# Four-layer graph network on one core: layer 2's normalisation moves from VectorE to ScalarE, under new due times

## The chip, the cores and the metric

The kernel runs on one core of one Trainium2 chip. The metric is device time in microseconds (us) of one execution. The engines are TensorE (PE in the profile; PEld is its weight load), VectorE (DVE), ScalarE (ACT), GpSimd (POOL) and the DMA queue of SyncE (SP).

## What is computed

There are 16 graphs ("batches") of 1024 nodes with 128 features, and an integer adjacency matrix for each. Four layers follow, each behind a layer norm with ReLU and with a residual sum. Cut to what matters here:

```python
# layer 0: two products with the row-softmaxed transposed adjacency, two batch norms over all batches
h = relu(layernorm(x));  x = x + L0(h, adj, ...)
# layer 1: graph attention
h = relu(layernorm(x));  Wh = h @ W.T
e = leaky_relu((Wh @ a_src)[:, :, None] + (Wh @ a_dst)[:, None, :], 0.2)
x = x + softmax(where(adj == 0, -inf, e)) @ Wh
# layer 2: attention by dot products of the nodes, weighted by one vector for each edge type
h = relu(layernorm(x))
e = leaky_relu(einsum('bid,bjd,dk->bkij', h, h, A), 0.2)   # the type in adj picks k
x = x + softmax(scores) @ h
# layer 3: graph attention like layer 1, with elu on its result
```

The layer norm is `(x - m) / sqrt(v + 1e-5)` over the 128 features of a node. Layer 0 needs statistics over all batches, so it is finished for all of them before layer 1 can start for any. Layers 1 to 3 are independent from batch to batch.

## The kernel before

Nodes lie on the 128 partitions, so a batch is 8 blocks of 128 nodes. `first_layer`, `load_weights` and `norms` make up the first stage (some 370 us), `plain_layers` the second, with layers 1 to 3 of all batches. `general_stack` is a second branch for other edge types and is not taken with these inputs.

The order of the work is not written by hand. Each function registers steps with a planner (`Plan`): an engine, a guessed cost in us, the tiles that it reads and writes, and the closure that issues its instructions. `Plan.attempt` lists the steps along a modelled timeline: an engine takes, among the steps that could start within `WITHIN` us of the earliest, the one with the lowest rank, and the rank is the batch's due time minus the length of the longest path behind the step. `Plan.emit` then issues all steps in that order. A due time belongs to a batch, and there are two lists: `L0_DUES` for the first stage and `DUES` for the second. They were found by search. Tiles come from small pools ("rooms"); a step that opens a room takes the one that has been free longest. Each engine runs its instructions in the order of issue, so whatever waits holds up everything behind it on the same engine.

The steps of a batch in `plain_layers`, with their lines before the change:

- Load `gt_rows`, `x` and the adjacency `at` (L855, L844, L841). Three batches kept from the first stage have theirs already. There are four `at` tiles: at0 to at2 and atc0. The last part of layer 0 is added by L882, L887 and L891.
- `norm(scaled)`: statistics of the nodes (L904), aggregates (L910), then on GpSimd `va = var + eps` and `rs = va ** -0.5` (L915, L916). For layers 1 and 3 (`scaled` false) the nodes are centred with ReLU on ScalarE by L929, with the negated mean (L912) as a bias column; the factor `rs` is applied later. For layer 2 (`scaled` true) they are centred and scaled on VectorE by L926. TensorE turns the blocks (L933), ScalarE copies them out of PSUM (L936; with ReLU in layer 2).
- `gat(layer, ext)` for layers 1 and 3: a product with the weights (L1004), scores (L1009), exponentials (L1017). The scores of the nodes are turned into a row (L1024), copied by L1027, sent to DRAM by L1030 and fetched from there into all partitions (`ub`, L1033). For layer 1 of the three kept batches L1042 and L1046 spread them without the round trip. L1060 writes the values `v`. Eight weighings of 128x1024 follow on VectorE (L1068), each into one of ten `q` tiles (named xg6 to xg15), and eight product steps on TensorE (L957).
- Layer 2: `ha` from the turned nodes (L1081), the values by a ReLU of `y` (L1084). Row block by row block there are dots on TensorE (L1100), two exponentials each on ScalarE (L1108, L1104), the larger of both (L1118) and a mask (L1121) on VectorE. Only the upper triangle is computed; the lower one is turned (L1132) and masked (L1136). Then the products (L957).
- Layers 1 and 2 end with reciprocals of the sums (L975), a scaling on ScalarE (L981) and the residual (L993). Layer 3 ends with L1150, L1156 and two joins (L1160, L1162), and the store (L1170).

Of the kernel before, what the change touches and what calls it, by code (L numbers as in the profile page):

```python
# [14 lines left out]
AF = mybir.ActivationFunctionType  # L15
ALU = mybir.AluOpType
# [23 lines left out]
    419.5, 419.5,  # L40
], 0.1
DUES, WITHIN = [
    18.0, 41.8, 62.8, 59.8, 76.6, 100.4, 120.4, 141.2, 164.8, 183.8, 204.1, 225.0, 245.7, 269.5, 265.9, 272.2,
], 0.05
GAT_LIMIT = 30.0
DOT_KEEP = 60.0
DOT_LIMIT = 110.0
# [16 lines left out]
class Plan:  # L64
# [11 lines left out]
    def room(self, kind):  # L76
        return Room(kind)
# [132 lines left out]
def groups_of(n, k):  # L210
    return [range(a, min(a + k, n)) for a in range(0, n, k)]
# [576 lines left out]
def plain_layers(tc, q_tiles, x, out, adj_t, gt_rows, u_rows, ident, ident_h, mhalf, gat1, gat3, edge, shift,  # L788
                 kcs, q9_all, rows9, held, kept):
    nc = tc.nc  # L790
# [7 lines left out]
    with ExitStack() as ctx:  # L798
# [31 lines left out]
        room = plan.room  # L830

        def batch(b):
            seat = room("seat")

            def step(engine, us_, run, reads=(), writes=(), moved=0, also=()):
                plan.step(engine, us_, run, reads, writes, moved, b, (seat, *also))
# [12 lines left out]
            X = [(xr, n) for n in range(NB)]  # L849

            def xs(n, m=None):
                return xr.ap.rearrange("p (k d) -> p k d", d=D)[:, n if m is None else slice(n, m), :]
# [44 lines left out]

            def norm(scaled):
                st, mv, va, rs, y, gt = (room(k) for k in ("st", "mv", "col", "col", "y", "gt"))
                nm = None if scaled else room("col")  # L900
                for ns in TRI:
                    def stats(ns=ns):
                        for n in ns:
                            nc.vector.bn_stats(st.ap[:, n, :], xs(n))  # L904

                    step("dve", 0.2 * len(ns), stats, [X[n] for n in ns], [(st, n) for n in ns])

                def aggregate():
                    for n in range(NB):
                        nc.vector.bn_aggr(mv.ap[:, n, :], st.ap[:, n, :])  # L910
                    if not scaled:
                        nc.vector.tensor_scalar_mul(nm.ap, mv.ap[:, :, 0], -1.0)  # L912

                def power():
                    nc.gpsimd.tensor_scalar_add(va.ap, mv.ap[:, :, 1], LN_EPS)  # L915
                    nc.gpsimd.tensor_tensor(rs.ap, va.ap, mhalf, ALU.pow)  # L916

                step("dve", 0.7, aggregate, [(st, n) for n in range(NB)], [mv] if scaled else [mv, nm])
                step("pool", 2.1, power, [mv], [va, rs])
                for js in groups_of(NB, 4):  # L920
                    ps = room("ps")

                    def centre(js=js):
                        for n in js:
                            if scaled:
                                nc.vector.tensor_scalar(y.ap[:, n, :], xs(n), mv.ap[:, n, 0:1],  # L926
                                                        rs.ap[:, n : n + 1], ALU.subtract, ALU.mult)
                            else:
                                nc.scalar.activation(y.ap[:, n, :], xs(n), AF.Relu, bias=nm.ap[:, n : n + 1])  # L929

                    def turn(js=js, ps=ps):
                        for k, n in enumerate(js):
                            nc.tensor.transpose(ps.ap[:, k * P : (k + 1) * P], y.ap[:, n, :], ident)  # L933

                    def relu(js=js, ps=ps):
                        nc.scalar.activation(gt.ap[:, js[0] * P : (js[-1] + 1) * P], ps.ap,  # L936
                                             AF.Relu if scaled else AF.Copy)

                    if scaled:
                        step("dve", 0.84, centre, [X[n] for n in js] + [mv, rs], [(y, js[0])])  # L940
                    else:
                        step("act", 1.0, centre, [X[n] for n in js] + [nm], [(y, js[0])])
                    step("pe", 0.44, turn, [(y, js[0])], [ps], also=[gt])
                    step("act", 0.54, relu, [ps], [(gt, js[0])])
                return y, gt, rs
# [50 lines left out]

            def gat(layer, ext):
                y, gt, rs = norm(False)
                sc, ex, er, v, ub = (room(k) for k in ("tri", "tri", "col", "v", "ub"))
                parts = [room("ps") for _ in TRI]  # L1000
# [74 lines left out]
            finish(gat(1, gat1))  # L1075

            y, ht, _ = norm(True)
            ha, h1 = room("gt"), room("h1")

# [597 lines left out]
```

## Time and profile before

| | us |
|---|---|
| median of 3 runs | 1424.29 (1423.61 to 1425.9) |
| the profiled execution | 1423.44 |
| its span in the profile | 1421.6 |
| TensorE busy | 1373.0 |
| VectorE busy | 1100.7 |
| ScalarE busy | 794.2 |
| GpSimd busy | 358.9 |

The profile is of one execution. Its span leaves out 1.84 us of the device time. A line such as L957 is a line of the kernel before. Matmuls are pipelined and their ends are modelled, so the mean duration of one is longer than the distance from one to the next: a product step of layers 1 to 3 has 16 records and takes 1.79 us in an unbroken run. The groups give "busy, mean duration of one", then the idle time of the engine just ahead of them and what ended most of it. The waits give "engine and tile that waited, line <- who released it: us in total, times, longest".

### The profile page before, as it was taken

How to read it: one execution, taken by the hardware profiler on the slowest of the kernel's cores; microseconds unless marked ns; L12 is line 12 of the kernel's file. 1: busy time of each engine (PE TensorE's matmuls, PEld its weight loads, DVE VectorE, ACT ScalarE, POOL GpSimd, SP SyncE). 2: the span in 40 equal slices, each digit the busy share in tenths (PEclk: the TensorE clock that was granted, in tenths of full speed). 3: DMA queues.
4: the chain of work that ended last, by engine and by line, in shares of the span. 5: the costliest groups of instructions: out<-in, count | busy, mean ns of one | idle time of the engine just before them, and what ended most of it. 6: DMA issues, size and time to landing. Idle time of an engine off the chain costs nothing.

```text
span 1421.6 us, 30420 instructions
## 1 busy us (share of the span) xinstructions
PE 1373.0 (97%) x11710; PEld 1262.9 (89%) x11710; DVE 1100.7 (77%) x3148; ACT 794.2 (56%) x2123; POOL 358.9 (25%) x469
## 2 busy tenths in 40 slices
PE   4999999999999999999999999999999999999997
PEld 3889899899898898998899898998989998998897
DVE  4877666454688889887889788887888798977786
ACT  3766766666545645636374645546374655346643
POOL 7877676562210110201011101101011111020000
PEclk9999999999999999999999999999999999999999
DMA  9999887870300002121111112021221110000011
GB/s 157 146 186 170 116 167 149 112 99 7 119 2 16 31 31 75 46 90 60 46 60 46 64 41 75 31 80 47 84 60 60 60 46 31 31 1 16 16 44 65
DMA packets 56379, 99.05 MB, mean 70 GB/s; under 512 B 6328, under 2 KB 45600, under 8 KB 52896
## 3 DMA queue, kind: packets, MB, share of 16 engines
q1 hardware_dynamic: 37504, 79.17, 15.8%
q0 software_dynamic: 18720, 17.83, 14.5%
q8 instruction: 94, 1.54, 0.4%
q14 instruction: 61, 0.50, 0.1%
HBM read 118.37 MB, written 28.95 MB: 104 GB/s over the span
## 4 chain that ended last, share of the span: by engine, by line
PE 82%; DVE 8%; ACT 4%; POOL 2%; DMA 2%; issue 1%; DVEq 0%; ACTq 0%; POOLq 0%
PE psc L957 43%; PE psc L1100 7%; PE psa L499 7%; PE psa L459 7%; PE gram L352 4%; PE psc L1004 3%; PE psc L1132 3%; PE psc L933 2%; PE psa L418 2%; PE psc L882 1%; DVE xg L1068 1%; DMA a<-in_adj_dram 1%; DVE eu L1118 1%; ACT y L929 1%; POOL hv L398 1%
## 5 line engine op out<-in xcount | busy, mean ns | idle before, releaser
L957 PE MATMUL psc<-v,xg 128*128 128x129 f32 x4096 | 482.6, 275 | 1.3 <-DVE xg L1068 1.2
L957 PEld LDWEIGHTS psc<-v,xg 128*128 128x128 f32 x4096 | 471.7, 192 | 13.1 <-issue 7.3
L957 PEld LDWEIGHTS psc<-h,xg 128*128 128x128 f32 x2048 | 239.1, 192 | 16.9 <-DVE xg L1136 8.9
L957 PE MATMUL psc<-h,xg 128*128 128x129 f32 x2048 | 247.9, 276 | 3.8 <-DVE xg L1136 3.3
L915 POOL TENSOR_SCALAR col<-mv 128x8 f32<-128x8 f32 x48 | 20.9, 434 | 868.1 <-DVE mv L910 800.8
L1068 DVE SCALAR_TENSOR_TENSOR xg<-ub,tri,at 128x1024 f32<-128x1024 f32 x176 | 217.5, 1276 | 4.3 <-DMA at<-adj_t 2.9
L1108 ACT ACTIVATE eu<-psc,edge_shift 128x512 f32<-128x512 f32 x192 | 113.6, 592 | 173.5 <-PE psc L1100 173.0
L426 ACT ACTIVATE at<-psa 128x1024 fp8e4<-128x1024 fp8e4 x128 | 131.2, 1033 | 45.1 <-PE psa L418 43.3
L1100 PE MATMUL psc<-gt,gt 128*128 128x512 f32 (+3 forms) x384 | 150.9, 492 | 5.3 <-DVE xg L1136 4.0
L1118 DVE SCALAR_TENSOR_TENSOR eu<-e,edge_shift,eu 128x1024 f32<-128x1024 f32 (+7 forms) x128 | 104.0, 812 | 38.0 <-ACT e L1104 36.8
L459 PE MATMUL psa<-hv,a 128*128 128x257 f16 x1024 | 120.7, 277 | 3.3 <-DVE hv L401 3.3
L499 PE MATMUL psa<-rv,at 128*128 128x259 f16 x1024 | 120.0, 275 | 2.7 <-DVE g L506 2.2
L459 PEld LDWEIGHTS <-a 128*128 128x128 fp8e4 x1024 | 101.4, 99 | 19.1 <-issue 3.5
L499 PEld LDWEIGHTS <-at 128*128 128x128 fp8e4 x1024 | 99.6, 98 | 19.1 <-issue 3.6
L929 ACT ACTIVATE y<-xg,col 128x128 f32<-128x128 f32 x256 | 79.1, 400 | 65.1 <-DVE col L912 65.1
L1104 ACT ACTIVATE e<-psc,edge_shift 128x512 f32<-128x512 f32 x192 | 113.6, 592 | 0.0
L1068 DVE SCALAR_TENSOR_TENSOR xg<-ub,tri,atc 128x1024 f32<-128x1024 f32 x80 | 99.2, 1275 | 6.0 <-DMA ub<-u_rows 3.8
L1156 ACT ACTIVATE y<-psc,col 128x128 f32<-128x128 f32 x256 | 69.2, 419 | 56.5 <-DVE col L1150 56.3
L471 POOL TENSOR_SCALAR rv<-r,cola 128x128 f16<-128x128 f32 x128 | 82.0, 650 | 61.2 <-DVE r L467 61.0
L981 ACT ACTIVATE y<-psc,col 128x128 f32<-128x128 f32 x256 | 71.9, 394 | 45.3 <-DVE col L975 39.2
L916 POOL TENSOR_TENSOR col<-col,mhalf 128x8 f32<-128x8 f32 x48 | 94.1, 1961 | 4.0
L1060 ACT ACTIVATE v<-psc,col 128x128 f32<-128x128 f32 x256 | 72.4, 394 | 26.6 <-DVE col L1020 22.8
(209 smaller groups left out, 1941.9 us busy)
## 6 DMA issues: line engine op xcount, KB each, us to landing
a<-in_adj_dram POOLq DMA_DIRECT2D x128, 128.0 KB, 7.2
ub<-u_rows SPq DMA_DIRECT2D x29, 512.0 KB, 4.0
xb<-in_x_dram SPq DMA_DIRECT2D x27, 512.0 KB, 6.8
adj_t<-at SPq DMA_DIRECT2D x13, 1024.0 KB, 4.9
at<-adj_t SPq DMA_DIRECT2D x8, 1024.0 KB
out_dram<-y SPq DMA_DIRECT2D x15, 512.0 KB, 3.9
gt_rows<-xg SPq DMA_DIRECT2D x13, 512.0 KB, 5.6
xg<-gt_rows SPq DMA_DIRECT2D x13, 512.0 KB, 3.9
```

Of the source, the lines that this page charges most:

```text
L426: nc.scalar.activation(at.ap[:, i, :], ps.ap.bitcast(F8)[:, t::2], AF.Square, saturate=False, accum_out=sums.ap[:, i : i + 1])
L459: nc.tensor.matmul(ps.ap[:, : 2 * D + 1], block[:, i % 2 :: 2], hv.ap[:, j, :], start=(j == 0), stop=(j == NB - 1))
L471: nc.gpsimd.tensor_scalar_mul(rv.ap[:, i, 0:D], r.ap[:, i, :D], rc.ap[:, i : i + 1])
L499: nc.tensor.matmul(ps.ap[:, :W2], at.ap[:, i, j * P : (j + 1) * P], rv.ap[:, i, :], start=(i == 0), stop=(i == NB - 1))
L916: nc.gpsimd.tensor_tensor(rs.ap, va.ap, mhalf, ALU.pow)
L929: nc.scalar.activation(y.ap[:, n, :], xs(n), AF.Relu, bias=nm.ap[:, n : n + 1])
L957: nc.tensor.matmul(acc[g].ap[:, k * V1 : (k + 1) * V1], weights[m].ap[:, n * P : (n + 1) * P], values.ap[:, m, :], start=(m == 0 and k == ...
L1068: nc.vector.scalar_tensor_tensor(q[m].ap, ub.ap, ex.ap[:, m, 1:2], at.ap[:, m, :], ALU.max, ALU.mult)
L1100: nc.tensor.matmul(ps.ap[:, : len(c)], ha.ap[:, m * P : (m + 1) * P], ht.ap[:, m * P + c[0] : m * P + c[-1] + 1], start=True, stop=True)
L1104: nc.scalar.activation(e.ap[:, c[0] : c[-1] + 1], ps.ap[:, : len(c)], AF.Exp, bias=shift[:, 0:1], scale=1.0 - SLOPE)
L1108: nc.scalar.activation(eu.ap[:, ROW[m] + c[0] : ROW[m] + c[-1] + 1], ps.ap[:, : len(c)], AF.Exp, bias=shift[:, 1:2], scale=SLOPE)
L1118: nc.vector.scalar_tensor_tensor(t, e.ap[:, :wide], shift[:, 2:3], t, ALU.max, ALU.mult)
```

## The change

In layer 2's norm, a small VectorE operation (`offset`, 128x8) computes `-mean * rs`. The nodes are then centred and scaled by ScalarE, with this as a bias column and `rs` as a scale column, instead of by VectorE's `tensor_scalar`. The step's place in the planner goes from `"dve"` at 0.84 us to `"act"` at 1.0 us, and a step of 0.17 us for the offset is new. `DUES` holds other numbers, and `WITHIN` goes from 0.05 to 0.1. The first stage's due times are the same.

```diff
 DUES, WITHIN = [
-    18.0, 41.8, 62.8, 59.8, 76.6, 100.4, 120.4, 141.2, 164.8, 183.8, 204.1, 225.0, 245.7, 269.5, 265.9, 272.2,
-], 0.05
+    -27.7, 9.3, 14.4, 25.7, 73.9, 96.1, 117.5, 139.4, 159.2, 182.2, 201.8, 221.8, 234.9, 284.6, 296.8, 299.1,
+], 0.1
...
-                nm = None if scaled else room("col")
+                nm = room("col")
...
+                def offset():
+                    nc.vector.scalar_tensor_tensor(nm.ap, mv.ap[:, :, 0], -1.0, rs.ap, ALU.mult, ALU.mult)
+
                 step("dve", 0.7, aggregate, [(st, n) for n in range(NB)], [mv] if scaled else [mv, nm])
                 step("pool", 2.1, power, [mv], [va, rs])
+                if scaled:
+                    step("dve", 0.17, offset, [mv, rs], [nm])
...
                             if scaled:
-                                nc.vector.tensor_scalar(y.ap[:, n, :], xs(n), mv.ap[:, n, 0:1],
-                                                        rs.ap[:, n : n + 1], ALU.subtract, ALU.mult)
+                                nc.scalar.activation(y.ap[:, n, :], xs(n), AF.Identity, bias=nm.ap[:, n : n + 1],
+                                                     scale=rs.ap[:, n : n + 1])
                             else:
                                 nc.scalar.activation(y.ap[:, n, :], xs(n), AF.Relu, bias=nm.ap[:, n : n + 1])
...
                     if scaled:
-                        step("dve", 0.84, centre, [X[n] for n in js] + [mv, rs], [(y, js[0])])
+                        step("act", 1.0, centre, [X[n] for n in js] + [nm, rs], [(y, js[0])])
```

## The prediction

> **What bounds the kernel now.** I read the page's busy shares first.
>
> ```profile
> PE 1373.0 (97%) x11710; PEld 1262.9 (89%) x11710; DVE 1100.7 (77%) x3148; ACT 794.2 (56%) x2123; POOL 358.9 (25%) x469
> ```
>
> TensorE (PE) is busy for 97% of a span of 1421.6 us. Neither engine that the change touches is the bound. What it can win is the time in which PE stands. The windows by stage show where that is: the first layer ends near 362 us, the three later layers fill the rest.
>
> ```profile
> 362.00:400.00 38.00, 35.10 (x331) 34.22 (x331) 29.18 (x134) 24.52 (x68) 10.26 (x20) 0.96 0.33 112
> 600.00:700.00 100.00, 96.87 (x808) 90.74 (x808) 80.27 (x201) 47.29 (x134) 9.02 (x8) 1.00 0.21 69
> 1364.00:1421.60 57.60, 50.40 (x449) 50.19 (x449) 41.93 (x67) 21.72 (x81) 0.00 (x0) 0.97 0.16 57
> ```
>
> The columns are length, then busy time of PE, weight load, DVE, ACT, POOL. From 400 to 1300 us, PE stands 15.2 us in nine windows of 100 us, while DVE is busy 753.6 of 900 us (84%) and ACT 53%. The stretches 362 to 400 and 1300 to 1364 add 2.9 and 1.1 us. The last 7.2 us are the tail behind the last product. The view of PE's waits says who holds it up.
>
> ```profile
> PE psc L1100 <- DVE xg L1136: 4.0, 5, 1.2
> PE psc L957 <- DVE xg L1136: 3.3, 7, 1.1
> PE psc L1132 <- DVE xg L1136: 2.0, 2, 1.1
> PE psc L957 <- DVE xg L1068: 1.2, 3, 0.5
> ```
>
> In the later layers DVE accounts for 11.8 us of waiting (these four rows, and 1.3 us in smaller ones), ACT for 4.3 us. In the chain of waits a product step of 16 records takes 1.79 us when it follows another and 2.05 us when it starts after a wait, so some twenty stalls cost another 0.26 us each, about 5 us. The ceiling is therefore 15.2 + 2.9 + 1.1 + 5 = 24 us, 1.7%.
>
> **Part 1: the eight centring operations of layer 2 go from DVE to ACT.** The groups by line and shape:
>
> ```profile
> L926 DVE TENSOR_SCALAR y<-xg,mv,col 128x128 f32<-128x128 f32 x128 | 34.8, 341 | 6.4 <-POOL col L916 6.4
> L929 ACT ACTIVATE y<-xg,col 128x128 f32<-128x128 f32 x256 | 79.1, 400 | 65.1 <-DVE col L912 65.1
> L463 ACT ACTIVATE t<-psa,level,cola 128x129 f32<-128x129 f32 x128 | 54.6, 460 | 42.2 <-PE psa L459 28.4 <-DVE cola L435 8.9 <-DVE r L467 3.9
> L912 DVE TENSOR_SCALAR col<-mv 128x8 f32<-128x8 f32 x32 | 5.5, 172 | 1.1
> ```
>
> DVE loses 128 operations, 34.8 us in all (0.272 us each). It gains 16 of 128x8, priced by L912: 16 x 0.172 = 2.8 us. Net -32 us: 1101 becomes 1069, and its share from 400 to 1300 us falls from 84% to 81%. ACT gains 128. Below, one costs what L929 costs, with a bias column alone: 79.1/256 = 0.309 us. Above, it costs what L463 costs, with bias and scale columns, though from PSUM and 129 wide: 54.6/128 = 0.427 us. Two columns are what the new operation has, so I take 0.40: +51 us (40 to 55), 794 becomes 845, 59%. A step of four takes 1.6 us instead of 1.09 us.
>
> The Trainium skill, "ScalarE: Activation LUTs", section "What ACT_TABLE_LOAD costs", speaks against the change: it gives an ACTIVATE 186 ns + 0.833 ns an element, about 93 ns more for each per-partition column, and an overlap of 93 ns between neighbours. By that page one new operation would be an estimated 0.39 us, dearer than the 0.272 us it replaces, and ACT's sum +49 us; no row here shows a two-column ACTIVATE from SBUF.
>
> A change of function table is not added: Identity, Square, Copy, Relu and Exp all run now, and the trace has one table load of 1.28 us; the built program has one too.
>
> **Part 2: the new wait.** The offset waits in DVE's queue for GpSimd's power (0.43 + 1.96 us after the aggregates), as the first centring did; that wait cost DVE 6.4 us in 6 places and I leave it at that. Queued behind it are weighings (L1068) and masks. The path from aggregates to the layer's node transposes grows by 0.17 us, two semaphore hops of some 0.05 us, and 0.5 us of slower step: 0.7 to 0.8 us for a batch. The cover is the PE work that the order puts between the last product of layer 1 and those transposes. I counted it in the built order of both programs at the durations of the profile: 14 to 43 us in all batches but two. The first has 9.8 us against a path of some 8.1 (0.17 reciprocal, 2.2 scaling, 0.4 add, 0.5 statistics, 0.64 aggregates, 2.4 power, 0.17 offset, 1.6 centring); in the fourth the pairing is ambiguous. So I cost it at nothing; without cover it would be 16 x 0.75 = 12 us. In return the layer's values (L1084) follow centring on the same engine.
>
> **Part 3: the due times, which move everything after the first layer.** PE's instructions are the same 10985, in another order. Four things in the built orders can be priced.
>
> First, the adjacency buffers. Before, the third batch held in at2 is not weighed until 83% of DVE's later work is done, so the other 15 share three buffers, and between the last reading of one batch and the first of the next DVE has 1.6 to 4.8 us of work. The reload takes longer, and stands in the chain:
>
> ```profile
> 763.17 6.39 DMA at<-adj_t
> ...
> 769.65 1.30 DVE xg L1068
> ...
> 770.99 2.05 PE psc L957 x16
> ```
>
> Afterwards all four rotate and the gap is 28 to 80 us of DVE work. DVE's 5.1 us of waits for adjacency go.
>
> Second, the row of scores (L1027, L1030, L1033). It goes to DRAM and back: fetch issued some 1.25 us after the send (752.58, 753.81 us), landing median 4.0 us (3.3 to 6.2), so 5.2 us, up to 6.3 at 1351 us. Before, DVE had 9 to 99 us of other work between in all but two of 29 cases. Afterwards 14 of 29 have under 6.3 us, and the sum that is missing is 26 us. DVE is not always busy, so a good part is covered by its other waits: between 5 us (today's waits for that row are 5.2 us) and 26 us, I take 12. Net of the 5.1 and 5.2 us of waits that it has today, DVE stands 2 us more, against 32 us less work.
>
> Third, tight places. Of 160 masked transposes (L1132, L1136), 15 had too little PE work before the product that reads them (3.3 us short in sum), afterwards 11 (2.1 us). From dots to the next row's transposes it was 4 places with 3.2 us, now 1 with 0.7. That is 3.7 us less of stalls that no timing hides.
>
> Fourth, the end. From the last score transposes but one to the first product with that row:
>
> ```profile
> 1350.93 0.12 PE psc L1024
> ...
> 1351.38 2.63 DMA u_rows<-ur
> ...
> 1354.03 3.63 DMA ub<-u_rows
> ...
> 1358.89 2.54 DVE xg L1068 x3
> ```
>
> It needs 8.0 us, and the new order has 6.2 us of PE work there: 1.8 us lost. Six joins of 0.55 us then lie among eight weighings, another 1.6 us. The old end lost 1.0 us of waits and two restarts, 1.5 us. So +1.9 us.
>
> **Sum.** DVE's relief acts on the 11.8 us that PE waits for it. The third point is part of those; I let the relief take 3 us more, as DVE's load falls by 32 of 1101 us and waits react more strongly than load. So -3.7 - 3 + 1.9, nothing for ACT, and +0.5 us for spill of the score row: -4.3 us. The profiled execution took 1423.44 us, 1.84 us beyond its span, and lies 0.85 us under the median 1424.29. 1424.3 - 4.3 = 1420.0 us.
>
> **The rivals.** *The score row becomes the bound* (slower). If DVE stands the whole 26 us and half reaches PE, that is +13 us, less 5 us of the gains: +8, 1432 us. It decides once DVE's waits for ub pass some 18 us, since then half of what exceeds today's cancels the gain. For it: 14 short places, and a queue in order, so that every mask behind the weighing waits too. Against it: PE's own cover from score transposes to product is 12 us or more in 26 of 29 cases. *ACT becomes late* (no change). The planner prices the new step at 1.0 us; at 1.24 to 1.7 us it is up to 22 us short over 32 steps, and layer 2's exponentials queue behind it. If PE's 4.3 us of waits for ACT double, the gain is gone: 1424 us. Against it, ACT is 59% busy. *The relief takes most of PE's waits* (faster): all 11.8 us and some restarts, -14 us, 1410 us; for it speak the four rotating buffers.
>
> **How the numbers follow.** A difference of 0.2%, 2.9 us, is about what a measurement of this kernel can tell from none. Forecast 0.33 and the stronger relief 0.18 are faster: 0.51. ACT late, 0.17, is within. The score row, 0.32, is slower. The range reaches from 1409 us, just past the stronger relief, to 1432 us, the score row's price; the forecast's own range, with its unknown costs, is 1415 to 1424 us.
>
> **What would show it.** Right: DVE near 1069 us, ACT near 845 us, PE's busy time unchanged within a few us, no wait of a weighing for adjacency, PE's waits for L1136 under 9 us. Wrong: waits of L1068 for ub above 18 us, ACT rows for exponentials among PE's releasers at more than 8 us, or a stall above 2 us around the last two score rows.

## The result, and the profile after

The changed kernel took 1427.95 us (median of 9 runs, 1426.3 to 1430.85) against 1423.5 us for the kernel before on the same chip (9 runs, 1420.62 to 1425.9): ratio 1.0034, 95% interval 1.0024 to 1.0044. It is slower by 4.5 us, where 4.3 us faster was forecast. The profiled spans differ by more, 1427.8 against 1421.6 us: the changed kernel's profiled execution took 1429.58 us, 1.6 us above its median, at a granted clock of 0.995 against 0.998. The changed kernel's lines stand 5 further down from L934 on (L957 is L962, L1068 is L1073, L1104 is L1109, L1118 is L1123, L1136 is L1141).

The busy shares:

```profile
PE 1374.9 (96%) x11710; PEld 1263.4 (88%) x11710; DVE 1072.4 (75%) x3036; ACT 844.9 (59%) x2251; POOL 374.5 (26%) x469
```

DVE went from 1101 to 1072 us and ACT from 794 to 845, close to what was worked out. The groups by line and shape give the new operations their prices:

```profile
L931 ACT ACTIVATE y<-xg,col,col 128x128 f32<-128x128 f32 x128 | 51.2, 488 | 21.8 <-DVE col L919 21.8
L919 DVE SCALAR_TENSOR_TENSOR col<-mv,col 128x8 f32<-128x8 f32 x16 | 2.5, 157 | 4.9 <-POOL col L916 4.9
```

One centring takes 0.400 us of ACT (51.2/128; 488 ns from its start to its end, overlapping its neighbour). So the work moved as planned, and 28 us less on DVE with 51 more on ACT cost time. The first line has one thing more: ACT stands 21.8 us just ahead of the centrings, waiting for the offset (L919). The view of PE's waits:

```profile
PE psc L1105 <- DVE xg L1141: 3.6, 5, 1.1
PE psc L1009 <- ACT gt L941: 2.2, 3, 1.2
PE psc L1029 <- DVE xg L1141: 1.7, 3, 0.8
PE psc L962 <- DVE xg L1126: 1.7, 2, 1.4
PE psc L962 <- DVE xg L1073: 1.3, 2, 1.0
PE psc L1137 <- DVE xg L1141: 1.2, 2, 0.7
```

The last steps of the masked tiles (L1141) hold PE up less, 7.3 us with a row of 0.8 us not shown, against 10.2 before (9.3 in the three rows that the prediction shows, 0.9 in two small ones). But two rows grew: PE's wait for L1126, the masking of a tile that itself waits for layer 2's exponentials (0.4 us before), and that of layer 1's and 3's product with the weights (L1009) for the copied nodes gt (none before). DVE's total hardly moved, 11.4 against 11.8 us; ACT's grew from 4.3 to about 6. In DVE's own waits the adjacency rows are gone, and the wait for layer 2's exponentials nearly doubled. First its row before the change, then two rows after it:

```profile
DVE eu L1118 <- ACT e L1104: 36.8, 35, 3.7
```

```profile
DVE eu L1123 <- ACT e L1109: 65.2, 48, 4.9
DVE xg L1073 <- DMA ub<-u_rows: 6.2, 6, 1.6
```

The windows show where the two kernels differ. Columns: length, busy time of PE, weight load, DVE, ACT, POOL, granted clock, DMA share, GB/s. Before:

```profile
0.00:400.00 400.00, 374.94 (x3533) 338.72 (x3534) 251.94 (x1069) 255.94 (x614) 251.58 (x381) 1.00 0.74 127
400.00:1300.00 900.00, 884.77 (x7239) 817.48 (x7238) 753.54 (x1875) 477.14 (x1321) 100.68 (x82) 1.00 0.14 49
1300.00:1345.00 45.00, 44.85 (x337) 39.03 (x337) 36.83 (x95) 27.80 (x71) 2.24 (x4) 1.00 0.04 13
```

After:

```profile
0.00:400.00 400.00, 374.27 (x3520) 338.24 (x3521) 252.01 (x1046) 249.99 (x593) 250.01 (x379) 0.99 0.74 127
400.00:1300.00 900.00, 885.89 (x7279) 820.55 (x7277) 724.22 (x1771) 526.61 (x1463) 115.51 (x82) 1.00 0.15 50
1300.00:1345.00 45.00, 42.76 (x296) 35.16 (x295) 33.36 (x87) 31.12 (x75) 3.95 (x4) 1.00 0.00 1
```

PE's idle time, length less busy: 25.7 against 25.1 us up to 400, 14.1 against 15.2 in the long middle, 2.2 against 0.15 from 1300 to 1345, and 10.8 against 8.2 from there to the end of the span. That is 4.3 us more, and PE's busy time is 2.0 us longer for the same instructions; together the 6.2 us of the two spans. In the middle, where a gain was expected, 1.1 us came; around the last batches 4.7 us went. This sets one order against another, so a loss in the middle can hide behind a gain there; the experiments below show that one does.

The chain of waits shows what a loss looks like (start, us, what):

```profile
1308.79 0.09 DVE col L919
...
1308.90 3.18 ACT y L931 x8
1312.09 0.13 ACT eu L1113
...
1312.57 0.67 ACT e L1109
1313.24 0.57 ACT eu L1113
1313.81 0.58 ACT e L1109
...
1314.42 1.30 DVE eu L1123
...
1320.33 1.72 PE psc L962 x13
```

The eight centrings of a batch run in one piece of 3.18 us, 1.59 us for a step of four. The exponentials of another batch (L1109, L1113) stand behind them in ACT's queue, DVE's masking (L1123, L1126) behind those, and PE's product waits: it stands 1.4 us up to 1317.1 and 0.7 us up to 1320.3, nearly all of the 2.2 us of this window. The timeline shows that the centrings also began late (start, length, what, and in brackets the idle time before):

```profile
1305.35 1.67 POOL L916 TENSOR_TENSOR col<-col,mhalf 128x8 f32<-128x8 f32 x1
1308.71 0.16 DVE L919 SCALAR_TENSOR_TENSOR col<-mv,col 128x8 f32<-128x8 f32 x1
1308.90 3.18 ACT L931 ACTIVATE y<-xg,col,col 128x128 f32<-128x128 f32 x8 [1.42 <-DVE col L919]
```

GpSimd had the factor `rs` ready at 1307.02. The offset, which is made from it, stood behind other work of DVE until 1308.71, and ACT stood idle.

### The profile page after: what moved, and what is told of

The parts are those of the page before. It is cut to its first block, busy times and chain, and to the rows that moved or that the text cites. A ratio compares the mean times of both kernels' runs of the same rounds, so it can differ in the third digit from the quotient of the medians.

```text
span 1427.8 us, 30396 instructions
## 1 busy us (share of the span) xinstructions
PE 1374.9 (96%) x11710; PEld 1263.4 (88%) x11710; DVE 1072.4 (75%) x3036; ACT 844.9 (59%) x2251; POOL 374.5 (26%) x469
## 4 chain that ended last, share of the span: by engine, by line
PE 73%; DVE 11%; ACT 7%; issue 4%; POOL 4%; DMA 1%; SPq 0%; DVEq 0%; POOLq 0%; ACTq 0%
PE psc L962 34%; PE psa L499 7%; PE psa L459 7%; PE psc L1105 7%; PE gram L352 4%; PE psc L1009 4%; PE psc L1137 3%; DVE xg L1073 3%; PE psc L938 2%; PE psc L882 2%; PE psa L418 2%; ACT y L931 1%; DVE eu L1123 1%; ACT eu L1113 1%; ACT e L1109 1%
## 5 line engine op out<-in xcount | busy, mean ns | idle before, releaser
L962 PE MATMUL psc<-v,xg 128*128 128x129 f32 x4096 | 481.9, 275 | 1.3 <-DVE xg L1073 1.3
L962 PEld LDWEIGHTS psc<-v,xg 128*128 128x128 f32 x4096 | 471.3, 192 | 12.9 <-issue 8.1
L915 POOL TENSOR_SCALAR col<-mv 128x8 f32<-128x8 f32 x48 | 33.5, 697 | 877.1 <-DVE mv L910 751.2
L962 PEld LDWEIGHTS psc<-h,xg 128*128 128x128 f32 x2048 | 238.3, 192 | 13.1 <-DVE xg L1141 5.6
L962 PE MATMUL psc<-h,xg 128*128 128x129 f32 x2048 | 246.5, 276 | 2.8 <-DVE xg L1126 1.7
L1073 DVE SCALAR_TENSOR_TENSOR xg<-ub,tri,at 128x1024 f32<-128x1024 f32 x192 | 237.6, 1276 | 4.6 <-PE psc L962 2.8
L1113 ACT ACTIVATE eu<-psc,edge_shift 128x512 f32<-128x512 f32 x192 | 113.8, 593 | 155.1 <-PE psc L1105 148.7
L1123 DVE SCALAR_TENSOR_TENSOR eu<-e,edge_shift,eu 128x1024 f32<-128x1024 f32 (+7 forms) x128 | 104.1, 813 | 65.9 <-ACT e L1109 65.2
L459 PEld LDWEIGHTS <-a 128*128 128x128 fp8e4 x1024 | 100.9, 99 | 19.5 <-issue 4.4
L1109 ACT ACTIVATE e<-psc,edge_shift 128x512 f32<-128x512 f32 x192 | 114.1, 594 | 0.0
L934 ACT ACTIVATE y<-xg,col 128x128 f32<-128x128 f32 x256 | 78.7, 402 | 54.6 <-DVE col L912 46.5
L1105 PEld LDWEIGHTS psc<-gt,gt 128*128 128x128 f32 x384 | 61.0, 191 | 28.4 <-issue 15.3
```

The costliest lines, as they stand in the source:

```text
L459: nc.tensor.matmul(ps.ap[:, : 2 * D + 1], block[:, i % 2 :: 2], hv.ap[:, j, :], start=(j == 0), stop=(j == NB - 1))
L962: nc.tensor.matmul(acc[g].ap[:, k * V1 : (k + 1) * V1], weights[m].ap[:, n * P : (n + 1) * P], values.ap[:, m, :], start=(m == 0 and k == ...
L1073: nc.vector.scalar_tensor_tensor(q[m].ap, ub.ap, ex.ap[:, m, 1:2], at.ap[:, m, :], ALU.max, ALU.mult)
L1105: nc.tensor.matmul(ps.ap[:, : len(c)], ha.ap[:, m * P : (m + 1) * P], ht.ap[:, m * P + c[0] : m * P + c[-1] + 1], start=True, stop=True)
L1109: nc.scalar.activation(e.ap[:, c[0] : c[-1] + 1], ps.ap[:, : len(c)], AF.Exp, bias=shift[:, 0:1], scale=1.0 - SLOPE)
L1113: nc.scalar.activation(eu.ap[:, ROW[m] + c[0] : ROW[m] + c[-1] + 1], ps.ap[:, : len(c)], AF.Exp, bias=shift[:, 1:2], scale=SLOPE)
```

## The experiments

Two theories stood at the start. **A**, the engine: centrings on ACT are late there, and what queues behind them gets late. **B**, the order: the new due times make a worse order. The plain comparison is each order with each assignment, each kernel beside the one before on the same chip (1423.4 us). In the kernel before, with its order kept instruction by instruction, the centring goes to ACT:

```
-  nc.vector.tensor_scalar(y.ap[:, n, :], xs(n), mv.ap[:, n, 0:1], rs.ap[:, n : n + 1], ALU.subtract, ALU.mult)
+  n or nc.vector.scalar_tensor_tensor(mv.ap[:, :, 1], mv.ap[:, :, 0], -1.0, rs.ap, ALU.mult, ALU.mult)
+  nc.scalar.activation(y.ap[:, n, :], xs(n), AF.Identity, bias=mv.ap[:, n, 1:2], scale=rs.ap[:, n : n + 1])
```

> The order of the kernel before, instruction for instruction on every engine, but layer 2's eight centring operations are issued on ScalarE, with the bias from one 128x8 VectorE operation issued just ahead of them (written over the variances, so that no tile is added). Only the engine of the operation differs from before. Theory A (the engine: centring stands in ScalarE's queue ahead of exponentials, and what VectorE gains it waits for ScalarE): +3 to +6 us over before, VectorE's waits for the exponentials rise from 37 us. Theory B (the new order costs the time, the move by itself helps or does nothing): -4 to 0 us against before.

Measured: 1438.59 us, ratio 1.0108 (1.0092 to 1.0123). And in the changed kernel, with its order kept, the centring goes back to DVE:

```
-  nc.scalar.activation(y.ap[:, n, :], xs(n), AF.Identity, bias=nm.ap[:, n : n + 1], scale=rs.ap[:, n : n + 1])
+  nc.vector.tensor_scalar(y.ap[:, n, :], xs(n), rs.ap[:, n : n + 1], nm.ap[:, n : n + 1], ALU.mult, ALU.add)
```

> The order of the changed kernel, but the eight centring operations are issued on VectorE at the same place (factor and offset as columns, multiply and add). Only the engine differs from the changed kernel. Theory A (the engine): at or under the kernel before, 1419 to 1424 us. Theory B (the order): as slow as the changed kernel or slower, +4 to +12 us over before, since VectorE has 35 us more to do in an order made without them; the tail behind the last product stays 1.4 us longer than before.

Measured: 1440.44 us, 1.0117 (1.0102 to 1.0133). Neither half alone is the change:

| | centring on DVE | centring on ACT |
|---|---|---|
| order of before | 1423.4 | 1438.6 |
| order of after | 1440.4 | 1428.0 |

Both halves cost more than either theory had expected of them. An order fits the assignment that it was made for. The move in the old order costs 15 us, and the new order has 10.7 of them back. In the old order PE's waits show rows that were not there or were small:

```profile
PE psc L1132 <- ACT gt L936: 2.6, 1, 2.6
...
PE psc L1004 <- ACT gt L936: 1.7, 1, 1.7
PE psc L933 <- ACT y L927: 1.7, 2, 1.2
PE psc L1100 <- ACT v L1060: 1.5, 3, 0.9
PE psc L933 <- ACT v L1060: 1.4, 1, 1.4
```

All name ACT, 59% busy as it is; L927 is the centring itself in that kernel. The new due times were also put into the kernel before, whose planner then makes a third order (only DUES and WITHIN change):

> The kernel before with the 16 new due times and the new WITHIN, nothing else; the planner makes a third order. Theory A (the engine): within 2 us of before, the list of due times is not the matter. Theory B (the order): +3 to +10 us, as this list suits the old step costs no better than the new ones.

Measured: 1453.97 us, 1.021 (1.0196 to 1.0224). This, too, is far beyond what was expected. Due times belong to one list of steps; this run says nothing on whether the order of after is good for after.

The fourth doubles the disputed cost in the changed kernel's own order: each centring of layer 2 is issued twice.

```
-  nc.scalar.activation(y.ap[:, n, :], xs(n), AF.Identity, ...)
+  for _ in range(2):
+      nc.scalar.activation(y.ap[:, n, :], xs(n), AF.Identity, ...)
```

> The changed kernel with each of layer 2's centring operations issued twice on ScalarE into the same tile: 51 us more work for ScalarE, 3.2 us a batch, nothing else changed. Theory A (ScalarE is late): the first 51 us cost some 4.5 us, so another 51 us cost at least as much again, +4 to +15 us over the changed kernel. Theory B (the order, ScalarE has room): 0 to +3 us over the changed kernel.

Measured: 1503.42 us, 1.0567 (1.0552 to 1.0581).

```profile
PE 1404.0 (94%) x11710; PEld 1285.3 (86%) x11710; DVE 1072.8 (71%) x3036; ACT 908.3 (60%) x2379; POOL 372.6 (25%) x469
```

63 us more of ACT cost 75 us, with ACT at 60% of the span, where at most 15 us had been expected. So ACT has next to no free time where the centrings lie. PE's idle time grew from 53 to 97 us and its busy time by 29 us.

That slope leads upwards; whether the *present* length costs anything needs a shorter one in the same order. First, one column less: a Copy with the scale alone, so that layer 2 leaves the mean out. The offset is still computed, and nothing waits for it.

```
-  nc.scalar.activation(y.ap[:, n, :], xs(n), AF.Identity, bias=nm.ap[:, n : n + 1], scale=rs.ap[:, n : n + 1])
+  nc.scalar.activation(y.ap[:, n, :], xs(n), AF.Copy, scale=rs.ap[:, n : n + 1])
```

> The changed kernel in its own order, with each centring of layer 2 issued on ScalarE as a Copy with the one scale column; the mean is left out of layer 2 (the offset is still computed, and not used). It makes the operation that was doubled in after_centre_twice shorter instead: one-column 128x128 operations took 394 to 400 ns against 488, so 128 of them take about 12 us off ScalarE (844.9 to 833). Theory P (late centrings set the time): the slope of after_centre_twice was 75 us for 63 us more of ScalarE work, so 12 us less bring 5 to 14 us: 1414 to 1423, DVE's wait at eu below 60 us. Rival Q': the slope exists only upwards, nothing is late at the present length: 1426 to 1429 as now.

Measured: 1422.9 us, 0.9995 (0.9987 to 1.0004). ACT fell by 12.4 us to 832.5, and the whole loss of the change was gone. (The kernel before took 1423.8 us beside this run and those that follow.) Then a step as one wide operation that scales by a constant, so that mean and deviation are both left out:

```
-  for n in js:
-      nc.scalar.activation(y.ap[:, n, :], xs(n), AF.Identity, ...)
+  nc.scalar.activation(y.ap[:, js[0] : js[-1] + 1, :], xs(js[0], js[-1] + 1), AF.Copy, scale=0.125)
```

> The changed kernel in its own order, with the four centrings of a step of layer 2 replaced by one ScalarE operation of 128x512 that scales by a constant (mean and deviation are left out of layer 2). Nearest rows: a 128x512 ACTIVATE took 0.6 us, so a step falls from 1.59 to about 0.6 and ScalarE from 845 to about 813. It is the third shorter or longer length of the same operation in the same order. Theory P (with the centring on ScalarE short, nothing of layer 2 is late, and what is left is what VectorE's relief of 30 us brings by itself): the curve 1503 (doubled), 1428, 1423 (one column) goes on flattening, 1417 to 1422. Rival S (the order itself holds the rest of the loss): stays at 1422 to 1424 with the same stalls left. Rival T (the relief of VectorE is worth much once ScalarE isn't late): under 1415.

Measured: 1423.04 us, 0.9995 (0.9985 to 1.0004). The centrings of both runs, after_scale_only first, and for the second the window in which it runs the products that the changed kernel runs from 1300 to 1345 us:

```profile
L931 ACT ACTIVATE y<-xg,col 128x128 f32<-128x128 f32 x128 | 39.5, 407 | 6.5 <-POOL col L916 6.5
```

```profile
L930 ACT ACTIVATE y<-xg 128x512 f32<-128x512 f32 x32 | 19.0, 653 | 0.0
```

```profile
1295.90:1339.00 43.10, 42.52 (x297) 35.35 (x296) 33.20 (x87) 29.07 (x69) 3.95 (x4) 1.00 0.00 1
```

PE stands 0.6 us there instead of 2.2, and the stretch is 43.1 us long instead of 45. With ACT busy 812, 832, 845 and 908 us the same order takes 1423.0, 1422.9, 1428.0 and 1503 us: a knee between 832 and 845. Below it nothing more is won, which is the time that rival S gave, although DVE has its 28 us less.

But the two runs change more than the length. The shorter operations don't read the offset, and the wide one doesn't read `rs` either: ACT's idle time ahead of the centrings falls from 21.8 to 6.5 and to 0.0 us. At the place shown above, after_scale_only has:

```profile
1300.04 1.67 POOL L916 TENSOR_TENSOR col<-col,mhalf 128x8 f32<-128x8 f32 x1
1302.06 2.44 ACT L931 ACTIVATE y<-xg,col 128x128 f32<-128x128 f32 x8
```

From the end of GpSimd's power to the end of the centrings it takes 2.8 us instead of 5.1. Of the 2.3 us, 0.7 are the shorter operations and 1.5 the offset that isn't waited for. So the 5 us are the cost of the centring on ACT, its length and its wait for the offset together, and no run here separates the two. The doubled run, which keeps the wait, shows that length costs by itself when there is more of it; a run with the one column that still waits for the offset would have told.

Nor does most of this cost lie around the last batches. The three kernels issue PE's instructions in the same order, so their starts can be compared one by one. Behind after_wide_scale, the changed kernel falls 3.6 us from 407 to 657 us, 0.9 from there to 1259, and 2.0 from there to 1359; behind after_scale_only 1.7, 1.1 and 2.0. Two rows of PE's waits in after_wide_scale, where L942 is L941 of the changed kernel and L1127 is L1126:

```profile
PE psc L1010 <- ACT gt L942: 1.7, 2, 1.2
PE psc L963 <- DVE xg L1127: 0.2, 1, 0.2
```

All waits for the copies gt are 1.7 us there instead of 3.0, those for the masking 0.2 instead of 1.7; 0.7 us of waiting for `ha` (L1086), which is made from gt, and 0.4 for the values v are gone. So what gets late on ACT behind the centrings is copies out of PSUM as well as exponentials. Without all this the order is worth 0.7 us, an interval that includes zero.

What relief of DVE is worth is measured in the kernel before, in its own order, with the same replacement on DVE:

```
-  for n in js:
-      nc.vector.tensor_scalar(y.ap[:, n, :], xs(n), mv.ap[:, n, 0:1], rs.ap[:, n : n + 1], ALU.subtract, ALU.mult)
+  nc.vector.tensor_scalar_mul(y.ap[:, js[0] : js[-1] + 1, :], xs(js[0], js[-1] + 1), 0.125)
```

> The kernel before in its own order, centring of layer 2 left on VectorE, with the four operations of a step replaced by one of 128x512 that scales by a constant (mean and deviation are left out of layer 2): VectorE is relieved by 14 us or more (a step of 1.03 to 1.09 us becomes 0.3 to 0.6), and nothing is added anywhere. It measures the term of the prediction that was 3 us for 32 us of relief. If relief is worth what was predicted, 1 to 3 us less: 1420.5 to 1422.5; if VectorE is not late in this order, 1423 to 1424 as before; if late centrings of VectorE hold PE as those of ScalarE did, 5 us or more: below 1418.5.

Measured: 1420.92 us, 0.9983 (0.9974 to 0.9992).

```profile
PE 1370.6 (97%) x11710; PEld 1262.4 (89%) x11710; DVE 1081.2 (76%) x3052; ACT 796.2 (56%) x2123; POOL 361.0 (25%) x469
```

19.5 us less on DVE, and next to nothing more on ACT, bring 2.9 us. DVE's 6.4 us of waiting for GpSimd ahead of the centrings are gone here too, so the 2.9 us are not all relief. That DVE's relief can be worth something is shown; how much of the 2.9 us is its share is not.

Last, whether the planner's price is why the order of after lets the centrings be late. The planner works with a price of 1.0 us for a step that takes 1.59. One kernel has the price set to 1.57 and due times searched for it; a control has the price of 1.0 and a search as long; a second control is the kernel before with a search as long.

```
-  step("act", 1.0, centre, [X[n] for n in js] + [nm, rs], [(y, js[0])])
+  step("act", 1.57, centre, [X[n] for n in js] + [nm, rs], [(y, js[0])])
```

> The changed kernel with the price of the new ScalarE step set to 1.57 us instead of 1.0 (eight centrings of layer 2 took 3.18 us in its trace, so a step of four 1.59), and with due times searched for that price. Instructions, engines and shapes are those of the changed kernel; only the order differs. Theory P (the order was made with too low a price, so exponentials of layer 2 come after centrings that are not finished when the plan says): DVE's wait at eu for the layer-2 exponentials falls from 65 us towards the 37 us of before, PE's waits fall by 5 to 10 us, time 1412 to 1423, below the 1428 of the changed kernel. Rival Q (ScalarE has no room for 51 us more, whatever the order): the wait stays at 60 us or above and the time at 1425 to 1432. Rival R (any longer search finds as much, the price is not the matter): this kernel and search_longer_old_price gain the same.

> The changed kernel with the new step's price left at 1.0 us and due times from a search as long as that of price_as_measured. Theory P: a better fit to a wrong price gains little on the chip, 1424 to 1434, and DVE's wait at eu stays above 55 us. Rival R: 1415 to 1423, like price_as_measured. Rival Q: 1425 to 1432.

> The kernel before (centring of layer 2 on VectorE, its own prices) with due times from an equally long search: what a longer search is worth without the move. Theory P: the prices of before were 0.2 us short on 32 VectorE steps and nearly right elsewhere, so a longer search may bring up to 6 us: 1416 to 1424. Rival R: a gain as large as that of price_as_measured over the changed kernel, 5 us or more.

> price_as_measured with the same shorter operation as after_scale_only (a Copy with the one scale column; the mean is left out of layer 2), ScalarE about 10 us less. In the changed kernel's order this brought 5.1 us. Theory P: in an order made with the price that the chip takes, less is late, and the same 10 us bring under 3 us: 1420.5 to 1423.5. Rival Q (ScalarE's load, not the price, holds the time): 5 us as there: 1417.5 to 1420.

| kernel | us | ratio to before |
|---|---|---|
| after | 1428.0 | 1.0034 (1.0024 to 1.0044) |
| search_longer_old_price | 1425.3 | 1.0010 (1.0001 to 1.0018) |
| price_as_measured | 1423.5 | 0.9999 (0.9991 to 1.0008) |
| price_as_measured_scale_only | 1421.0 | 0.9984 (0.9975 to 0.9993) |
| before_search_longer | 1421.4 | 0.9981 (0.9972 to 0.9989) |

The longer search alone brought 2.7 us to the moved kernel and 2.4 us to the one before. The right price brought 1.8 us more (1425.3 to 1423.5), and the two intervals overlap, so that the share of the price is likely but not shown; the 1423.5 us lie between the ranges of theory P and rival Q. The shorter operation brought 2.5 us in the order with the right price, half of the 5.1 us that it brought in the order of after, just beyond the intervals. That may speak for the price, but ACT's idle time ahead of the centrings fell by 5 us there (21.2 to 16.3), where it fell by 15 us in the order of after. Theory P missed one thing outright: DVE's waits for the exponentials did not fall.

```profile
DVE eu L1123 <- ACT e L1109: 66.4, 45, 4.5
```

This row of price_as_measured is that of after (65.2 us), in a kernel 4.5 us faster; after_wide_scale has 60.4 us at 1423 us. So the sum of these waits does not tell the cost. What costs is the few of them that PE's next product has no other work to cover, and the chain shows them where the sum does not.

At equal search, one search each, the move does not pay: 1421.4 us without it, 1423.5 with it and the right price, 1425.3 with the price of 1.0. before_search_longer is the one full computation that beat the kernel before. Its edit is the list of due times and `WITHIN`:

```
+DUES, WITHIN = [
+    -310.8, -273.6, -205.5, -289.5, -213.6, -221.7, -166.4, -201.4, 157.1, 170.5, 164.9, 121.8, 235.8, 248.8, 240.7, 248.9,
+], 0.02
```

## Why the prediction was wrong

**The step that failed is the cost of the centring on ACT, put at nothing twice: "nothing for ACT" in the sum, and "I cost it at nothing" for the new wait in part 2.** The forecast put 51 us on ACT and a step of four at 1.6 us, and both came true (50.7 us, 1.59 us). It then costed them at nothing, with the 59% share as the reason. after_scale_only and after_wide_scale show 5 us for the centring's length and its wait for the offset together. The rival "ACT becomes late" named the mechanism, with the planner's price and layer 2's exponentials; it was weighed at 0.17 because of an engine's mean share. Its price of 4.3 us came near by luck: it was to come from a doubling of PE's waits for ACT, and these went from 4.3 to 6.0 us.

**Part 2 asked about the wrong cover.** It counted PE work between layer 1's last product and the batch's own node transposes, and no row of PE's waits names the centring (L931). What became late in the chain above is another batch: the exponentials queued behind the eight centrings on ACT. "Who is queued behind" was asked of DVE's queue at the offset, and not of ACT's. And the path that it added up (0.17 us for the offset and two hops) leaves out that the offset itself queues: at 1307 us it began 1.7 us after its input was there, and ACT stood for offsets 21.8 us in 11 places.

**Part 1** was right within 4 us: DVE 1072 (1069), ACT 845 (845), and one operation 0.400 us. The estimate of 0.39 us that the prediction worked out from the Trainium skill, "ScalarE: Activation LUTs", section "What ACT_TABLE_LOAD costs", agrees with that. PE's work is the same, as said, but its records are 11710 in both profiles; the prediction's 10985 is in neither.

**Part 3, the gains: -6.7 us for relief and tight places did not come in this order.** PE's waits named DVE fell from 11.8 to 11.4 us. The rows of L1141 lost 2.9 us, but L1126 gained 1.3, and L1086 and L1032, which held up nothing before, took 1.1. Even with ACT's lateness taken out, the order with DVE relieved by 29 us is at -0.7 us, not at -4.3. In the order of before, 19.5 us less on DVE brought 2.9 us, with a wait for GpSimd gone as well; that waits react more strongly than load, no run shows. The two gains were counted on short places and on load, and other places became short in exchange: weighings now stand 3.7 us for the products to free their tiles, for one. What each of these cost, no run here separates.

**The score row, 12 us of DVE's waits, was far too dear:** 6.2 us were measured, against 5.2 before. That DVE was late enough to hide the rest is likely, and not shown. The leading rival (1432 us) was therefore wrong in its mechanism. **The adjacency buffers** were right: their 5.1 us of waits are gone, and PE got nothing for it that can be seen. **The end** was put at +1.9 us, and PE stands 2.6 us more from 1345 us on. The size is about right, the reasons only in part: the tail behind the last product grew from 7.2 to 8.5 us, the first product with the last score row but one lost nothing, where 1.8 us were forecast; 1.2 us went just ahead of it in a wait for gt (L941) that was not in the sum; and the six joins among the weighings cost PE 1.0 us, where 1.6 were forecast.

**The markers were ill chosen.** "PE's waits for exponentials above 8 us" did not fire, although late exponentials held PE up around 1317 us: PE waits for DVE's tile, and DVE for the exponential, so that PE's releaser is DVE. And "waits for L1136 under 9 us" did come true in a slower kernel.

## What to carry to other kernels

An engine at 59% can still be the one that is late: what counts is what stands behind the moved work in its queue at that moment, and what the moved work itself has to wait for. Doubling and shortening the moved operation in an unchanged order measures it directly, if the stand-in keeps the waits of the original; one that drops an input measures two things at once. To find where a cost lies, compare kernels with the same order instruction by instruction. A searched order is part of the assignment that it was searched for; compare two assignments at equal search and with prices measured on the chip, or the search is what is measured. Follow a wait back more than one engine before naming its cause: the sum of waits at one hop neither showed the cause nor followed the time.

## What the runs showed of the hardware

More standing came with longer work of PE itself. With each centring doubled, PE's 11710 instructions took 1404.0 us instead of 1374.9, and the granted clock was 0.976 over the span against 0.995; in one stretch of that kernel:

```profile
400.00:900.00 500.00, 469.25 (x3677) 429.54 (x3677) 367.66 (x892) 303.30 (x809) 59.23 (x42) 0.96 0.11 40
```

PE stands 30.8 us of 500 there at a clock of 0.96, where the changed kernel stood 14.1 of 900 at 1.00. So 29 of the 74 us by which the span grew lay in slower or restarted instructions, and not in idle time; which of the two, the rows do not separate. On ACT, a 128x128 operation from SBUF with two columns took 0.400 us (51.2/128), with one column 0.309 us (39.5/128), and four of them as one 128x512 operation without a column 0.594 us (19.0/32) instead of 1.59. On DVE the wide operation, by a constant, took 0.394 us (12.6/32) against four of 0.272 (34.8/128) with two columns.
